# The longest neighbour lists of a graph kernel, laid out by rank, with a limit of places for each rank

## Chip, core and metric

The kernel runs on one core of one Trainium2 chip. The metric is the time of one execution on the device in microseconds (us), the median of several runs. Lower is better.

## What is computed

There are B = 16 graphs of N = 1024 nodes with C = 64 channels, a weighted adjacency `adj` (16, 1024, 1024) in float32 that is mostly zero, and a node mask (all ones). The reference, cut to what matters:

```python
# layer 0
h = relu(layernorm(x));  x = x + (adj @ h) / max(adj.sum(2), 1)
# layer 1
h = relu(layernorm(x))
nb = (adj > 0) without the diagonal;  m = nb.sum(-1)           # m: length of a node's list
skip = where(m > 10, (m + 1) // 2, 1)                          # every skip-th neighbour is removed
removed = nb & (skip > 1) & (rank_in_row % skip == 0)
valid = adj_with_self_loops without (removed or removed^T)
agg = sum of 1/4, 1/2, 1/4 times the quantiles .25, .5, .75 of h over the valid neighbours, by channel
x = x + relu((h + agg) @ W1 + b1) @ W2 + b2
```

The costly part is the quantile: for every node the feature rows of its neighbours (its list) have to be fetched and sorted in each of 64 channels. Lists are short on average and a few are long: the expected length of node i falls as 1 / sqrt(1 + i); the longest list of the inputs has 78 neighbours, and from the 512th of a graph on they have 3 or fewer.

## The kernel before, in words

**Two paths.** `list_path` does the whole work with lists. It also collects overflow flags (`ovf`): a list longer than the places set aside for it raises one. At the end the flags are reduced to `go`, and if it is set `dense_path` does everything again without lists. The trace shows `list_path` alone.

**Stages of `list_path`.** For each graph the rows of `adj` are loaded, layer 0 is computed (transposes and products on TensorE), and the neighbours are listed: `listing` finds the 8 largest keys in each of 4 segments of a row. `endings` (L737) then sorts the nodes of a graph by the length of their lists, only roughly: up to 15 by the length itself, and above that by the classes of `STEPS` = (16, 20, 24, 32) (L30, L764: one VectorE instruction for each step and graph). Inside a class the nodes keep their order. From the class counts each node gets a place `pos`, and a GpSimd indirect DMA (`scatter`) writes its record of 164 floats to the sorted table `srt` of its group of four graphs: 8 scatters for each graph, 128 in all. The four graphs are mixed in runs of eight ranks: eight ranks of the first graph, then eight of the second, and so on.

**Short jobs.** `group` (L1102) takes 32 tiles of 128 sorted nodes of four graphs. Tiles of the same limit form a `Job` (L831). A job fetches, for each tile t and each place k, one neighbour's row (66 floats) for each of the 128 nodes with one indirect DMA: `gather(A[:, k + 1, t, :], table, idx[:, t, k:k+1])`; `A` is named `places`. Then VectorE sorts the places with a min/max network, ScalarE and VectorE weight them, TensorE adds them up and runs the two matrix products, and one scatter for each tile writes `out`. The last group runs in the long stage (names with `last_`).

**Long lists.** The 32 longest lists of each graph (the first tile of each group) do not fit the record of 32 keys. `long_lists` (L1239) takes them again as four tiles l = 0 to 3 of 128 lists: 8 ranks of each of the 16 graphs, ranks 0 to 7 in l = 0. `LONG` (L40) = (88, 31, 24, 20) is the number of places of each tile, the same for all its partitions. For a tile, in this order: the records are loaded into `lS` (four DMAs on SP, one for each group, 32 partitions each, L1251); `lnodes` is made from them on VectorE; the rows of `adj` are gathered (`lat`); VectorE lists and sorts the keys (`lfound`, `lkeys`), raises the flags, applies the skip rule (`dilation`) and writes the fetch indices `lidx`; a `Job` with one tile fetches the K places from `whole`, the table of all graphs. For l = 0 the job's tile is `lplaces0` [128, 89, 1, 66], with 88 fetches of 128 rows each. Partition p holds graph p >> 3, rank p & 7. A list shorter than 88 fetches a row of huge numbers for its empty places.

**What sets the order.** All instructions go through `Plan` (L234 to L333). Each stream of work (`endings`, `group`, `Job.run` and so on) is a generator that names the engine it wants next and the time from which it can go on; `Plan.run` always takes the stream that could start first by a clock of its own and by rank. The clock has costs by engine, written into `note` (L271): a gather or scatter counts 1.27, a VectorE memset 0.04, a DMA issue on SP 0.05, whatever their size. The order on each engine is thus fixed when the program is built, and an engine that waits holds up all that stands behind the waiting instruction in its queue. On GpSimd (POOL) and VectorE (DVE) this order is the program's order.

The trace puts nearly every instruction on line L228, the helper that records it; instructions are found by the names of their tiles.

Of the kernel before, what the change touches and what calls it, by code (L numbers as in the profile page):

```python
# [9 lines left out]
F32 = mybir.dt.float32  # L10
BF = mybir.dt.bfloat16
HF = mybir.dt.float16
I32 = mybir.dt.int32
U8 = mybir.dt.uint8
AF = mybir.ActivationFunctionType
OP = mybir.AluOpType
AX = mybir.AxisListType

P = 128
# [4 lines left out]
HUGE = 1.0e30  # L24
# [2 lines left out]

GROUPS = (4, 4, 4, 4)
NSEG = 4
STEPS = (16, 20, 24, 32)  # L30
CLS = 15 + len(STEPS) + 1


# [4 lines left out]
)  # L38
CAPS2 = [CAPS[1]] + CAPS[2::2]
LONG = (88, 31, 24, 20)  # L40
LSEG = 8
LCAPS = (24, 16, 16, 16)
LSUB = 8
# [190 lines left out]
class Plan:  # L234
# [25 lines left out]
    def room(self, name, bufs):  # L260

        tiles = self.slots.get(name, ())
        if len(tiles) < bufs:
            return 0.0
        old = tiles[-bufs]
        return INF if self.users[old] else max(self.used.get(old, 0.0), self.ready.get(old, 0.0))

    def at(self, *tiles):
        return max(self.ready.get(t.tensor.name, INF) for t in tiles)
# [104 lines left out]
def list_path(ctx, tc, x, adj, nodemask, w1, b1, w2, b2, out, go):  # L374
    nc = tc.nc
    B, N, C = x.shape
# [5 lines left out]
    NG = len(GROUPS)  # L382
    FIRST = [sum(GROUPS[:g]) for g in range(NG)]
    TS = N + 1
# [59 lines left out]
    nc.vector.tensor_scalar(toff, which, float(TS), None, op0=OP.mult)  # L444
    noff = consts.tile([P, 3], F32, name="noff")
    nc.vector.tensor_scalar(noff, which, float(N), None, op0=OP.mult)
    caps4 = consts.tile([P, NTAU], F32, name="caps4")
    for t, cap in enumerate(CAPS):
        nc.vector.memset(caps4[:, t:t + 1], float(cap if t else N))
# [362 lines left out]
    def gather(dst, src, idx):  # L812
        nc.gpsimd.indirect_dma_start(
            out=dst, out_offset=None, in_=src,
            in_offset=bass.IndirectOffsetOnAxis(ap=idx, axis=0),
        )
# [14 lines left out]
    class Job:  # L831
# [1 line left out]


        def __init__(self, pool, n, T, keys, idx, node, mask, nodes_i, table, S, g, name="places",
                     bufs=4, rank=0, half=False, begin=0.0):
            self.__dict__.update(locals())
            self.short = pool is gat

        def run(self):  # L840
            n, T, pool, short = self.n, self.T, self.pool, self.short

            since = []
            own = () if short else (lambda rank: self.rank,)
            pace = lambda: since[0] + 1.3 * len(since) if not short else 0.0
            yield "POOL", lambda: max(
                self.begin, at(self.idx), room(self.name, self.bufs), room("S", 4) if short else 0.0
            ), *own
            A = self.A = new(pool, [P, n, T, W], F32, self.name, self.bufs, users=1)
            progress["ahead"] += T * (n - 1)  # L850
            if short:
                mine = self.S
                self.S = new(pool, [P, T, C], F32, "S", 4, users=1)
                nc.sync.dma_start(self.S, mine[:, :, :C])
                self.residual = mine[:, :, X1:R0]
            for t in range(T):
                for k in range(n - 1):
                    if t or k:
                        yield "POOL", pace, *own
                    since.append(since[0] if since else plan.clock["POOL"])  # L860
                    plan.own = plan.clock["POOL"]
                    gather(A[:, k + 1, t, :], self.table, self.idx[:, t, k:k + 1])
                    plan.own = None
                    progress["ahead"] -= 1
            yield "DVE", lambda: max(
                at(A, self.S) + SLACK,
                *(room(("" if short else "l") + name, 2 if short else 1) for name in ("gone", "wu")),
            ), self.soon
            yield from self.sort()
# [369 lines left out]
    def long_lists(pool):  # L1239

        yield "DVE", always
        rev = new(pool, [P, N], HF, "rev", 1)
        nc.vector.tensor_scalar(rev, col_f, -1.0, float(N), op0=OP.mult, op1=OP.add)
        for l, K in enumerate(LONG):
            n = K + 1
            yield "SP", always
            S = new(pool, [P, 1, RW], F32, "lS", 4)
            for g in range(NG):
                lo, num = FIRST[g] * LSUB, GROUPS[g] * LSUB
                at0 = l * num + (0 if GROUPS[g] == 4 else HP)  # L1250
                nc.sync.dma_start(  # L1251
                    S[lo:lo + num, 0, :], srt[g][at0:at0 + num, :]
                )
            node = S[:, 0, RW - 2:RW - 1]
            mask = S[:, 0, RW - 1:RW]
            yield "DVE", lambda: at(S) + SLACK if progress["begun"] == NG else INF
            nodes = tiny.tile([P, 1], F32, name="lnodes")
            nc.vector.tensor_tensor(nodes, node, noff[:, 1:2], OP.add)
            nodes_i = new(pool, [P, 1], I32, "lnodes_i", 4)
            nc.vector.tensor_copy(nodes_i, nodes)  # L1260
            yield "POOL", lambda: max(at(nodes_i), room("lat", 1))
            full = new(pool, [P, N], F32, "lat", 1)
            gather(full, adj_rows, nodes_i)
            yield "DVE", lambda: at(full)
            nc.vector.scalar_tensor_tensor(
                full, col_f, node, full, op0=OP.not_equal, op1=OP.mult
            )
            key = new(pool, [P, N], HF, "lkey", 1)
            nc.vector.scalar_tensor_tensor(key, full, 0.0, rev, op0=OP.is_gt, op1=OP.mult)

            found = new(pool, [P, LSEG, max(LCAPS)], HF, "lfound", 1)
            found = found[:, :, :LCAPS[l]]
            last = [None] * LSEG
            for r in range(LCAPS[l] // 8):
                for s in range(LSEG):
                    if s % 4 == 0:
                        yield "DVE", always
                    top = found[:, s, 8 * r:8 * r + 8]
                    seg = key.rearrange("p (q s) -> p s q", s=LSEG)[:, s, :]
                    if r:  # L1280
                        nc.vector.match_replace(
                            out=seg, in_to_replace=last[s], in_values=seg, imm_value=0.0
                        )
                    nc.vector.max(out=top, in_=seg)
                    last[s] = top
            rounds = -(-K // 8)
            keys = new(pool, [P, 1, rounds * 8 + 8], F32, "lkeys", 4)
            over = new(pool, [P, 2], F32, "lover", 1)
            nc.vector.tensor_reduce(over[:, 0:1], found[:, :, LCAPS[l] - 1], AX.X, OP.max)
            for r in range(rounds + 1):  # L1290
                if r % 4 == 0:
                    yield "DVE", always
                top = keys[:, 0, 8 * r:8 * r + 8]
                nc.vector.max(out=top, in_=found)
                if r < rounds:
                    nc.vector.match_replace(
                        out=found, in_to_replace=top, in_values=found, imm_value=0.0
                    )
            nc.vector.tensor_tensor(over[:, 1:2], over[:, 0:1], keys[:, 0, K:K + 1], OP.max)
            nc.vector.tensor_scalar(  # L1300
                ovf[:, NG + l:NG + l + 1], over[:, 1:2], 0.0, None, op0=OP.is_gt
            )
            keys = keys[:, :, :K]
            pos = new(pool, [P, K], F32, "lpos", 4)
            m = tiny.tile([P, 1], F32, name="lm")
            nc.vector.tensor_scalar(
                pos, keys[:, 0, :], 0.0, None, op0=OP.is_gt, op1=OP.add, accum_out=m
            )
            skip = dilation(m, mask, 1)
            for e in range(2):  # L1310
                nc.vector.tensor_scalar(pos, place1[:, :K], skip[:, e, :], None, op0=OP.not_equal)
                nc.vector.tensor_tensor(keys[:, 0, :], keys[:, 0, :], pos, OP.mult)
            based = tiny.tile([P, 1], F32, name="lbased")
            nc.vector.tensor_scalar(based, toff[:, 1:2], float(N), None, op0=OP.add)
            idx = new(pool, [P, K], I32, "lidx", 4)
            index_of(idx, keys[:, 0, :], -1.0, based)

            yield "DVE", lambda: 0.0 if progress["groups"] == NG else INF
            job = Job(
                pool, n, 1, keys, idx.unsqueeze(1), node, mask, nodes_i, whole, S, NG,  # L1320
                *(("lplaces", 2) if l else ("lplaces0", 1)), -600 + l, begin=at(whole),
            )
            plan.add(job.run(), 100 * NG + l)

# [309 lines left out]
```

## Time and profile before

| | |
|---|---|
| time, median of 3 runs | 1953.29 us (1948.59 to 1955.87) |
| profiled execution: span from the first to the last instruction | 1511.0 us |
| median less span: what lies around the span | 442.3 us |
| busy in the span: PE, DVE, ACT, POOL | 49%, 79%, 54%, 63% |
| indirect DMAs on POOL | 931 |
| of them: `lplaces`, all four long tiles | 163, first at 953.8 us |
| first step of the long sort (`lrem` of l = 0) | 1096.5 us |
| mean granted TensorE clock | 0.699 |

The page has busy time by engine, and busy tenths in 40 slices of 37.8 us each. "Busy" for an indirect DMA on POOL is the time in which POOL makes the transfer; the data land later. In a row of the timeline the columns are start, duration, engine, line, operation, output<-input, and in brackets the idle time of the engine just before, with what ended it. "issue" there means that the engine waited for nothing that the profile shows. In a row of the waits the columns are the total, the number of times, and the longest. In a row of the windows each engine has its busy us and, in brackets, its instructions.

### The profile page before, as it was taken

Reading aid. Unit: us, or ns where it says so; the run is one execution under the profiler, and the core shown is the slowest. Engines: PE = TensorE matmul, PEld = TensorE weight load, DVE = VectorE, ACT = ScalarE, POOL = GpSimd, SP = SyncE. Lnnn points to the kernel's source line nnn. Section 1 sums busy time; section 2 is a strip of 40 time slices with the busy share of each in tenths; the row PEclk is TensorE's granted clock in tenths of the full one; section 3 lists DMA queues with packets and bytes.
Section 4 is the critical chain, followed back from the end, with each engine's and each line's share of the span. In section 5 each row is a group of like instructions: output and inputs, shape, how many; then the busy total and the mean of one; then the engine's idle time right before and its main releaser. Section 6 shows DMA issues by size and latency. Waiting matters only on the chain. (4 is left out here: it accounts for less than half of the span.)

```text
span 1511.0 us, 15983 instructions
## 1 busy us (share of the span) xinstructions
PE 738.8 (49%) x3192; PEld 464.7 (31%) x3192; DVE 1191.3 (79%) x4104; ACT 816.4 (54%) x2789; POOL 957.2 (63%) x1154
## 2 busy tenths in 40 slices
PE   4778777327877556567667620024000123228542
PEld 2434334214544233343444320012000122216432
DVE  6777798997899779859869869893059999986875
ACT  7989878557879457757975520201050223148341
POOL 0122227777678757757777787667777777765083
PEclk8889888658888777869688755555555565558765
DMA  5445665424355253355341242111111111211010
GB/s 177 150 142 168 163 210 160 123 73 114 101 162 152 59 174 94 99 126 161 94 140 31 60 101 68 50 37 28 30 26 23 28 28 40 44 33 22 2 25 13
DMA packets 135718, 133.36 MB, mean 88 GB/s; under 512 B 100756, under 2 KB 103444, under 8 KB 135492
## 3 DMA queue, kind: packets, MB, share of 16 engines
q1 hardware_dynamic: 102876, 90.79, 20.8%
q0 software_dynamic: 32736, 41.47, 11.2%
q14 instruction: 78, 0.64, 0.1%
q8 instruction: 28, 0.46, 0.1%
HBM read 112.90 MB, written 23.61 MB: 90 GB/s over the span
## 5 line engine op out<-in xcount | busy, mean ns | idle before, releaser
L228 POOL DMA_INDIRECT places<-tab,idx x372 | 370.2, 995 | 131.7 <-issue 101.8
L228 PE MATMUL pt<-ident,prod 128*128 128x128 f32 (+1 forms) x736 | 160.2, 377 | 517.8 <-DVE prod L228 241.2
L228 PEld LDWEIGHTS pt<-ident,prod 128*128 128x128 f32 (+1 forms) x736 | 129.3, 256 | 550.4 <-ACT prod L228 412.4
L228 PE MATMUL ps_small<-att,h 128*65 128x512 f32 x512 | 254.7, 644 | 27.3 <-ACT h L228 10.5
L228 POOL DMA_INDIRECT srt<-row,to x128 | 125.9, 984 | 165.8 <-ACT row L228 144.0
L228 PE MATMUL pt<-ident,at 128*128 128x128 f32 x1024 | 176.7, 320 | 96.0 <-ACT att L228 71.1
L228 POOL DMA_INDIRECT lplaces<-whole,lidx x163 | 167.2, 1026 | 55.6 <-issue 48.5
L228 DVE MAX8 rec<-sg 128x8 f16<-128x256 f16 x512 | 180.1, 414 | 4.4
L228 PEld LDWEIGHTS pt<-ident,at 128*128 128x128 f32 x1024 | 136.9, 164 | 143.5 <-ACT att L228 93.8
L228 ACT ACTIVATE sg<-at 128x1024 f16<-128x1024 f32 x128 | 134.8, 1054 | 75.0 <-DMA at<-in_adj_dram 65.7
L228 ACT COPY att<-pt 128x512 f32<-128x512 f32 x256 | 141.9, 582 | 20.7 <-PE pt L228 18.8
L228 POOL DMA_INDIRECT places<-tab,last_idx x124 | 123.8, 998 | 41.3 <-issue 35.0
L228 PEld LDWEIGHTS ps_small<-att,h 128*65 128x65 f32 x512 | 74.7, 151 | 161.9 <-issue 123.2
L228 ACT ACTIVATE places<-places,gone 128x64 f32<-128x64 f32 x496 | 123.5, 335 | 0.5
L228 ACT ACTIVATE prod<-places,w 128x64 f32<-128x64 f32 x213 | 54.1, 336 | 120.5 <-DVE w L228 120.5
L228 POOL DMA_INDIRECT out_dram<-y,nodes_i x93 | 91.8, 987 | 22.6 <-issue 15.1
L228 DVE TENSOR_TENSOR sg<-sg,keyed 128x1024 f16<-128x1024 f16 x128 | 87.2, 681 | 23.7 <-ACT sg L228 23.7
L228 ACT ACTIVATE gone<-gone 128x15 f32<-128x15 f32 (+9 forms) x40 | 8.2, 206 | 169.2 <-DVE ok L228 169.0
L228 DVE TENSOR_TENSOR long_other<-lplaces 128x512 f32<-128x512 f32 (+5 forms) x124 | 64.1, 555 | 29.1 <-ACT lplaces L228 28.9
L228 DVE TENSOR_TENSOR other<-places,other 128x64 f32<-128x64 f32 (+6 forms) x204 | 69.6, 341 | 5.9
L228 PE MATMUL ps_small<-ot,w_sb 128*128 128x128 f32 (+3 forms) x112 | 47.6, 513 | 44.2 <-DVE y L228 31.2
L228 DVE TENSOR_TENSOR places<-places,other 128x64 f32<-128x64 f32 (+2 forms) x208 | 62.3, 309 | 4.9
(231 smaller groups left out, 1670.8 us busy)
## 6 DMA issues: line engine op xcount, KB each, us to landing
at<-in_adj_dram SPq DMA_DIRECT2D x128, 512.0 KB
places<-tab,idx POOLq DMA_INDIRECT x372, 2.5
whole<-tab SPq DMA_DIRECT2D x4, 1057.0 KB
tab<-row SPq DMA_DIRECT2D x16, 264.0 KB
xt<-in_x_dram SPq DMA_DIRECT2D x16, 256.0 KB
lplaces<-whole,lidx POOLq DMA_INDIRECT x163, 2.4
srt<-row,to POOLq DMA_INDIRECT x128, 2.7
places<-tab,last_idx POOLq DMA_INDIRECT x124, 2.4
```

The costliest lines, as they stand in the source:

```text
L228: ins = getattr(self._engine, op)(*args, **kwargs)
```

## The change

1. `STEPS` gets two more classes, 40 and 52, so that the longest lists of a graph stand nearer to their order of length. `CLS` follows (20 to 22).
2. The tile of l = 0 is laid out by rank: partition p now holds graph p & 15, rank p >> 4. Its records are loaded with 32 DMAs of 4 partitions (one for each group and rank) in place of 4 DMAs of 32. New constants (`toff0`, `noff0`, `rcaps`) follow this layout.
3. `RCAPS` = (88, 82, 80, 54, 46, 44, 37, 35) is the limit of places of each rank. A list over the limit of its rank raises the flag.
4. The fetch of place k takes only the partitions of the ranks whose limit is over k: 128 for the first 35 places, 16 for the last six.
5. What is not fetched is filled by one memset of `lplaces0` from place 36 on (53 places of 66 floats for each partition). For this the tile is allocated in `long_lists` and handed to the job.

```diff
-STEPS = (16, 20, 24, 32)
+STEPS = (16, 20, 24, 32, 40, 52)
+RCAPS = (88, 82, 80, 54, 46, 44, 37, 35)
...
+    ranked = consts.tile([P, 2], I32, name="ranked")
+    nc.vector.tensor_scalar(ranked[:, 0:1], part, B - 1, None, op0=OP.bitwise_and)
+    nc.vector.tensor_scalar(ranked[:, 1:2], part, B.bit_length() - 1, None, op0=OP.logical_shift_right)
...
+    for r in range(1, LSUB):
+        nc.vector.tensor_scalar(
+            rstep, ranked[:, 1:2], float(r), float(RCAPS[r - 1] - RCAPS[r]), op0=OP.is_lt, op1=OP.mult
+        )
+        nc.vector.tensor_tensor(rcaps, rcaps, rstep, OP.add)
...
+            longest = self.name == "lplaces0"
...
-                    gather(A[:, k + 1, t, :], self.table, self.idx[:, t, k:k + 1])
+                    top = B * sum(cap > k for cap in RCAPS) if longest else P
+                    gather(A[:top, k + 1, t, :], self.table, self.idx[:top, t, k:k + 1])
...
-                nc.sync.dma_start(
-                    S[lo:lo + num, 0, :], srt[g][at0:at0 + num, :]
-                )
+                if l:
+                    nc.sync.dma_start(S[lo:lo + num, 0, :], srt[g][at0:at0 + num, :])
+                    continue
+                ranks = srt[g][at0:at0 + num, :].rearrange("(b r) w -> r b w", r=LSUB)
+                for r in range(LSUB):
+                    lo = r * B + FIRST[g]
+                    nc.sync.dma_start(S[lo:lo + GROUPS[g], 0, :], ranks[r])
...
+            A = None
+            if not l:
+                nc.vector.tensor_tensor(over[:, 0:1], m, rcaps, OP.is_gt)
+                nc.vector.tensor_tensor(
+                    ovf[:, NG:NG + 1], ovf[:, NG:NG + 1], over[:, 0:1], OP.max
+                )
+                A = new(pool, [P, n, 1, W], F32, "lplaces0", 1, users=1)
+                nc.vector.memset(A[:, min(RCAPS) + 1:, :, :], HUGE)
```

More of the change, by code (lines that the diff above doesn't have):

```diff
@@ L446, in list_path @@
     nc.vector.tensor_scalar(noff, which, float(N), None, op0=OP.mult)
+    ranked = consts.tile([P, 2], I32, name="ranked")
+    nc.vector.tensor_scalar(ranked[:, 0:1], part, B - 1, None, op0=OP.bitwise_and)
+    nc.vector.tensor_scalar(ranked[:, 1:2], part, B.bit_length() - 1, None, op0=OP.logical_shift_right)
+    toff0 = consts.tile([P, 1], F32, name="toff0")
+    nc.vector.tensor_scalar(toff0, ranked[:, 0:1], float(TS), None, op0=OP.mult)
+    noff0 = consts.tile([P, 1], F32, name="noff0")
+    nc.vector.tensor_scalar(noff0, ranked[:, 0:1], float(N), None, op0=OP.mult)
+    rcaps = consts.tile([P, 1], F32, name="rcaps")
+    nc.vector.memset(rcaps, float(RCAPS[-1]))
+    rstep = consts.tile([P, 1], F32, name="rstep")
+    for r in range(1, LSUB):
[3 more added lines that the diff above has]
+        nc.vector.tensor_tensor(rcaps, rcaps, rstep, OP.add)
     caps4 = consts.tile([P, NTAU], F32, name="caps4")
@@ L835, in __init__ @@
         def __init__(self, pool, n, T, keys, idx, node, mask, nodes_i, table, S, g, name="places",
-                     bufs=4, rank=0, half=False, begin=0.0):
+                     bufs=4, rank=0, half=False, begin=0.0, A=None):
             self.__dict__.update(locals())
@@ L846, in run @@
             yield "POOL", lambda: max(
-                self.begin, at(self.idx), room(self.name, self.bufs), room("S", 4) if short else 0.0
+                self.begin, at(self.idx), room("S", 4) if short else 0.0,
+                at(self.A) if self.A is not None else room(self.name, self.bufs),
             ), *own
-            A = self.A = new(pool, [P, n, T, W], F32, self.name, self.bufs, users=1)
+            A = self.A = (
+                new(pool, [P, n, T, W], F32, self.name, self.bufs, users=1)
+                if self.A is None else self.A
+            )
             progress["ahead"] += T * (n - 1)
@@ L1250, in long_lists @@
                 at0 = l * num + (0 if GROUPS[g] == 4 else HP)
-                nc.sync.dma_start(
-                    S[lo:lo + num, 0, :], srt[g][at0:at0 + num, :]
-                )
+                if l:
[5 more added lines that the diff above has]
+                    nc.sync.dma_start(S[lo:lo + GROUPS[g], 0, :], ranks[r])
+            toffs, noffs = (toff[:, 1:2], noff[:, 1:2]) if l else (toff0, noff0)
             node = S[:, 0, RW - 2:RW - 1]
@@ L1257, in long_lists @@
             nodes = tiny.tile([P, 1], F32, name="lnodes")
-            nc.vector.tensor_tensor(nodes, node, noff[:, 1:2], OP.add)
+            nc.vector.tensor_tensor(nodes, node, noffs, OP.add)
             nodes_i = new(pool, [P, 1], I32, "lnodes_i", 4)
@@ L1308, in long_lists @@
             )
+            A = None
[3 more added lines that the diff above has]
+                    ovf[:, NG:NG + 1], ovf[:, NG:NG + 1], over[:, 0:1], OP.max
+                )
+                A = new(pool, [P, n, 1, W], F32, "lplaces0", 1, users=1)
+                nc.vector.memset(A[:, min(RCAPS) + 1:, :, :], HUGE)
             skip = dilation(m, mask, 1)
@@ L1313, in long_lists @@
             based = tiny.tile([P, 1], F32, name="lbased")
-            nc.vector.tensor_scalar(based, toff[:, 1:2], float(N), None, op0=OP.add)
+            nc.vector.tensor_scalar(based, toffs, float(N), None, op0=OP.add)
             idx = new(pool, [P, K], I32, "lidx", 4)
@@ L1320, in long_lists @@
                 pool, n, 1, keys, idx.unsqueeze(1), node, mask, nodes_i, whole, S, NG,
-                *(("lplaces", 2) if l else ("lplaces0", 1)), -600 + l, begin=at(whole),
+                *(("lplaces", 2) if l else ("lplaces0", 1)), -600 + l, begin=at(whole), A=A,
             )
```

## The prediction

> **What bounds the kernel now.** I read the page's busy tenths first, to see where which engine is full, then busy time by windows around the long lists, then the waits of that window, then the timeline around the start of the long stage. On the page (40 slices of 37.8 us):
>
> ```profile
> DVE  6777798997899779859869869893059999986875
> POOL 0122227777678757757777787667777777765083
> ```
>
> Counted from 0, POOL stands at about 7 from slice 6 to 34. That is full: an indirect DMA is busy for 0.944 us and begins 1.25 us after the one before, the rest being 0.30 us of "issue" each time. So POOL sets the pace until the long stage. VectorE has one hole, in slices 27 to 29 (digits 3, 0, 5). The windows show it, and what comes behind it:
>
> ```profile
> 243.00:890.00 647.00, 404.47 (x1688) 249.33 (x1687) 536.00 (x1880) 440.59 (x1498) 477.21 (x591) 0.75 0.40 110
> 954.00:1096.50 142.50, 24.88 (x92) 16.07 (x92) 72.32 (x240) 19.66 (x73) 103.81 (x120) 0.54 0.15 37
> 1096.50:1511.00 414.50, 125.20 (x668) 100.75 (x668) 336.65 (x1107) 145.44 (x579) 265.87 (x291) 0.60 0.12 26
> ```
>
> The columns are PE, PEld, DVE, ACT, POOL. In the second row VectorE is busy for 72 of 142 us, in the third for 337 of 414. The wait that ends the hole, and what VectorE waits for after it (waits of VectorE from 1096 us on):
>
> ```profile
> DVE lrem L228 <- DMA lplaces<-whole,lidx: 50.1, 2, 48.9
> DVE long_other L228 <- ACT lplaces L228: 28.9, 9, 5.7
> DVE y L228 <- PE ps_small L228: 14.0, 3, 5.7
> DVE other L228 <- ACT places L228: 13.6, 3, 11.2
> ```
>
> Of the 50.1 us, 48.9 are one wait: the sort of l = 0 starts at 1096.5 us, when the last of its 88 fetches has landed. After that VectorE waits for ScalarE and TensorE and only 1.2 us for a fetch. So **the end is the arrival of l = 0 plus some 414.5 us of VectorE's queue**, and the change is worth what it does to that arrival, less VectorE work that it takes out of the 414.5. What fixes the arrival is the chain at the start of the stage (timeline, SP, DVE and POOL):
>
> ```profile
> 890.78 0.36 SPq L228 DMA_DIRECT2D last_recs<-srt  x1
> 891.19 9.82 SPq L228 DMA_DIRECT2D lS<-srt  x16
> 896.48 0.26 DVE L228 CAST last_nodes_i<-nodes 128x32 int32<-128x32 f32 x1
> 897.44 0.16 DVE L228 TENSOR_TENSOR lnodes<-lS,noff 128x1 f32<-128x1 f32 x1 [0.71 <-DMA lS<-srt]
> 952.51 0.94 POOL L228 DMA_INDIRECT lat<-in_adj_dram,lnodes_i  x1 [1.47 <-DVE lnodes_i L228]
> ```
>
> The records are loaded as soon as the last scatter to `srt` (ends 889.2) has landed; `lnodes` of l = 0 waits for its four loads (0.71 us more than for `last_recs`). From there VectorE runs without a gap (54.5 us) to the `lnodes_i` of l = 1 behind the indices of l = 0, and POOL waits for it (1.47 us) before the first fetch at 953.8.
>
> **Part by part.** All against the profiled execution, span 1511.0 us. The median of the runs is 1953.3, so 442.3 us lie around the span; I leave them as they are and add the change of the span to the median.
>
> *Order, +10.* The plan is built anew. By the order of instructions, 531 indirect DMAs stand on POOL up to the last `srt` scatter, against 523 before: eight more at 1.25 us. POOL's queue is the pace there. Cover would be POOL's named waits from 270 us to that scatter, 40 us (12.3 for y, 9.3 for `row`, 9.2 and 7.1 for ScalarE, 2.2): if the eight fall into them the term is 0, and these waits can come out 10 us longer or shorter in a new order.
>
> *Loads, +11.* 32 loads stand where 4 stood, and `lnodes` in the new order waits for all of them. The price of one issue on SP: (9.82 - 2.85) / 15 = 0.465 us in the `lS` row (its first takes 2.85), at the other end the short loads
>
> ```profile
> 3.12 1.20 SPq L464 DMA_DIRECT2D b_sb<-in_L_gnn_b_dram  x4
> ```
>
> at 0.30. At 0.40: 31 x 0.40 - 3 x 0.465 = 11.0 (bounds 7.9 and 13.0). Behind the waiting `lnodes` in VectorE's queue stand the listing of the last group, whose `drop` lets `whole` be written, and the whole listing of l = 0; POOL's `lat` waits for `lnodes_i` with 36 DMAs behind it. Those 36 take 45 us, VectorE's chain 54.5, so POOL catches up and the chain stays what sets the start.
>
> *Memset and flag, +3.4.* They stand in that same chain, ahead of the indices. Two tiny instructions at 0.2, and a memset of 53 x 66 = 3498 elements. Rows:
>
> ```profile
> L228 DVE MEMSET keys<- 128x512 f32 x3 | 1.5, 485 | 0.2
> L228 DVE MEMSET prod<- 128x320 f32 x4 | 1.3, 325 | 7.3 <-PE pt L228 7.3
> ```
>
> (485 - 325) / 192 = 0.83 ns an element, so 0.485 + 2986 x 0.00083 = 2.97 us. The fetches behind it have no further wait.
>
> *More scatters inside the fetches, +7.6.* Between the first and the last fetch of the tile POOL now has 20 scatters to `out`, before 14: 6 x 1.27. (Nine more short fetches stand ahead of the first one; they are in POOL's slack against the chain.)
>
> *Fetches, -10.* There are still 88, so what counts is whether one with fewer rows is shorter. Sum over the limits: 16 x 466 = 7456 rows in place of 11264, 3808 fewer, in 53 of the 88. No row of the trace has an indirect DMA of fewer than 128 rows. The nearest:
>
> ```profile
> L228 POOL DMA_INDIRECT lplaces<-whole,lidx x163: 940/944/1782, 953.8 to 1459.9; - x163
> L228 POOL DMA_INDIRECT lat<-in_adj_dram,lnodes_i x4: 942/942/960, 902.2 to 1001.6; - x4
> ```
>
> 264 bytes a row and 4096 bytes a row take the same 0.94, so bytes are not what it pays for; rows or a fixed part are. Below: nothing saved, 0. Above: all of the 0.944 by rows, 7.4 ns x 3808 = 28.1, and with the 0.30 of issue too, 37.1. I take 10, a third of 28: the rows nearest to it say only that the time does not move with the size. The Trainium skill speaks against the change here: "DMA: Bandwidth & Descriptors", section "Anatomy of one DMA — SWDGE (gpsimd) path", calls the descriptor generation small and says that many descriptors can be emitted before their cost shows. By it this term would be 0 and the sum 10 us higher; the trace, with one row count alone, can neither confirm nor deny it.
>
> *Work moved ahead of the arrival, -7.2.* In the new order one more short job (6 tiles of 2 places) and six `y` stand on VectorE before the sort of l = 0: 6 small instructions at 0.2, some 7 at 0.55, a 0.4, two at 0.18 and 6 `y` at 0.21, 7.2 us. They fill part of the 48.9 us hole.
>
> *Nothing.* 32 more step instructions (0.167 each, 5.3 us) and a tenth more elements in the class sums (about 1.3): hidden by POOL's pace; uncovered, 6.6. Nineteen small constants (3.6 us) at the start: mostly in VectorE's wait of 2.5 us for the first `adj`. The listing, sort and layers of l = 0 keep their shapes.
>
> Sum: 10 + 11 + 3.4 + 7.6 - 10 = +22 for the arrival, less 7.2 behind it: **+15, span 1526, time 1968 us**, 0.8% slower. The tail after the arrival has its own order (VectorE waits some 56 us there for ScalarE and TensorE); I give it 8 us either way.
>
> **Rivals.**
>
> *A fetch costs the same whatever its rows.* For it: bytes do not move it. Then the term of 10 is 0: +25, 1978.
>
> *A fetch is busy by its rows.* For it: 0.94 us is long beside POOL's bare instructions (0.12 for a one-element memset). Then -28 in place of -10: -3, 1950, no difference that a measurement of this kernel tells (its runs spread over 7 us; 0.5%, 10 us, is my bound).
>
> *The loads are hidden.* If `last_recs` or the engine's own queue is late by as much, `lnodes` loses nothing: +4, 1957, the same. Against it: `last_recs` came 1.2 us before `lnodes` could go, and nothing else stood between.
>
> *Faster.* One mechanism: the whole pitch of a fetch, issue included, goes by its rows. Place: the 53 shortened fetches; price 9.7 ns a row, 37 us; -12, 1941. It decides from a saving of 25 + 10 = 35 us on, 9.2 ns a row. Against it: the 0.30 of issue is the same ahead of every kind of indirect DMA.
>
> *The change does not hold on these inputs.* A list over its limit would run `dense_path`, with 16 x 64 x 8 x 18 matmuls; at the 0.32 us of the cheapest group of the page that is over 47 ms. From the reference's inputs the longest lists by rank in the new order are 78, 58, 51, 38, 38, 31, 31, 27, all under `RCAPS`.
>
> **How the numbers follow.** Forecast (saving 5 to 20) 0.45, of which 0.35 lies over +0.5%; fixed cost 0.22; by rows 0.12; hidden loads 0.08; faster 0.12; dense 0.01. So slower 0.35 + 0.22 + 0.01 = 0.58, same 0.10 + 0.12 + 0.08 = 0.30, faster 0.12. The range takes in a saving of 37 (1941) and of 0 with the order 10 us worse (1988): 1940 to 1990.
>
> **What would show it.** `lnodes` waits 10 to 13 us on the DMAs of `lS`; the last `srt` scatter ends near 899; the memset of `lplaces0` takes about 3 us; the busy time of the fetches of 48 and 16 rows against 0.944 decides among the rivals; `lrem` of l = 0 starts near 1118 and the span ends some 407 us later. The forecast is wrong if the last `srt` scatter comes early, if short fetches take under 0.6 us, or if the tail after `lrem` changes by over 10 us.

## The result, and the profile after

The kernel after takes 1964.2 us (median of 6 runs, 1959.7 to 1973.4) against 1953.2 us before (1948.6 to 1956.3): **ratio 1.006, 95% interval 1.0036 to 1.0085**, 11 us slower. The forecast was 15 us slower.

The size came out by chance, as the next lines show. Span and busy tenths of VectorE and POOL, from the page of the kernel after (a slice is now 49 us):

```profile
span 1959.0 us, 16074 instructions
...
DVE  7875945776653872756357736793100699885674
...
POOL 0122365454556546437453566467677114563152
```

This execution's time was 1960.8, so only 1.8 us lie around its span. The 442 us that the prediction "left around the span" are not there; POOL is not full from slice 6 to 34, and VectorE's hole is one weakness among many.

The experiments ran in three sets, each on one chip with the kernel before beside it, and the kernel before takes 1952.6 us on the first, 1985.0 on the second and 1517.2 on the third; so only ratios and stages within one set are compared. By their times, and by nothing else, the profile of before that the prediction read (span 1511) is counted with the third set, and the median that it was added to, with the runs of the kernel after above, with the first.

### The profile page after: what moved, and what is told of

It reads as the page before. It is cut to its first block, busy times and chain, and to the rows that moved or that the text cites. A ratio compares the mean times of both kernels' runs of the same rounds, so it can differ in the third digit from the quotient of the medians.

```text
span 1959.0 us, 16074 instructions
## 1 busy us (share of the span) xinstructions
PE 804.9 (41%) x3192; PEld 506.1 (26%) x3192; DVE 1204.9 (62%) x4158; ACT 832.6 (42%) x2791; POOL 939.6 (48%) x1158
## 4 chain that ended last, share of the span: by engine, by line
DVE 30%; ACT 18%; issue 16%; another core or an unknown queue 13%; PE 12%; POOL 6%; DMA 2%; SPq 1%; DVEq 0%; POOLq 0%; ACTq 0%
PE pt L229 6%; PE ps_small L229 6%; DVE other L229 5%; DVE places L229 5%; DVE long_other L229 4%; DVE lplaces L229 3%; ACT sg L229 3%; POOL lplaces L229 3%; ACT att L229 2%; ACT places L229 2%; ACT ln_sq L229 2%; DVE rec L229 2%; ACT lplaces L229 2%; POOL places L229 2%
## 5 line engine op out<-in xcount | busy, mean ns | idle before, releaser
L229 POOL DMA_INDIRECT places<-tab,idx x372 | 364.4, 980 | 242.9 <-issue 108.4
L229 PE MATMUL pt<-ident,prod 128*128 128x128 f32 (+1 forms) x736 | 172.8, 398 | 598.6 <-DVE prod L229 313.0
L229 PE MATMUL pt<-ident,at 128*128 128x128 f32 x1024 | 201.7, 350 | 267.2 <-ACT att L229 108.6
L229 PEld LDWEIGHTS pt<-ident,prod 128*128 128x128 f32 (+1 forms) x736 | 139.0, 274 | 633.8 <-ACT prod L229 408.7
L229 POOL DMA_INDIRECT srt<-row,to x128 | 126.1, 985 | 244.6 <-ACT row L229 208.7
L229 PEld LDWEIGHTS pt<-ident,at 128*128 128x128 f32 x1024 | 152.4, 180 | 317.3 <-ACT att L229 130.7
L229 POOL DMA_INDIRECT lplaces<-whole,lidx x163 | 155.9, 956 | 56.6 <-issue 48.4
L229 ACT COPY ot<-pt 128x128 f32<-128x128 f32 (+3 forms) x56 | 22.2, 397 | 200.6 <-remote 132.7
L229 DVE TENSOR_TENSOR sg<-sg,keyed 128x1024 f16<-128x1024 f16 x128 | 87.3, 682 | 12.5 <-ACT sg L229 9.3
L229 PE MATMUL ps_small<-ot,w_sb 128*128 128x128 f32 (+3 forms) x112 | 52.9, 564 | 76.9 <-ACT ot L229 41.3
```

Of the source, the lines that this page charges most:

```text
L229: ins = getattr(self._engine, op)(*args, **kwargs)
```

## Experiments

### e0: the kernel before, profiled again (first set)

No edit.

> The kernel before, unchanged, profiled again. The profile that the prediction read had a span of 1511 us, and the prediction left 442 us around it. If they do lie around the span, this profile again has a span near 1511, with lrem of l = 0 near 1096. The rival: that execution was one in which the waits that fill the timed runs did not occur; then the span here is within a few us of the time, about 1951, as in the profile of the kernel after (span 1959.0 in a run of 1960.8), lrem of l = 0 starts near 1400, and the chain holds 'issue' and 'remote' shares of over 10%.

Measured: 1947.6 us, span 1945.7. From its page:

```profile
span 1945.7 us, 15983 instructions
...
PE 798.3 (41%) x3192; PEld 503.5 (26%) x3192; DVE 1194.1 (61%) x4104; ACT 832.2 (43%) x2789; POOL 941.8 (48%) x1154
```

VectorE is busy for 1194 us here and for 79% of 1511, 1191 us, in the first profile: VectorE's work is the same, and the 435 us are idle time. (TensorE is busy 60 us longer, 798.3 against 738.8, at a mean granted clock of 0.641 against 0.699.) Part of the idle time stands ahead of instructions that wait for nothing on this core: "issue", or "remote", a release that the profile cannot name. Summed over the waits of the whole span, these two come to 482 us on ScalarE and 180 on VectorE in e0, and to none and 3 us in the first profile. The rest of VectorE's added idle time is longer waits for ScalarE and TensorE. The gaps show best in the 88 ScalarE activations that begin the sort of l = 0 (timelines of ScalarE; first the profile with a span of 1511, then e0):

```profile
1097.78 21.10 ACT L228 ACTIVATE lplaces<-lplaces,lgone 128x64 f32<-128x64 f32 x88
```

```profile
1389.73 5.59 ACT L228 ACTIVATE lplaces<-lplaces,lgone 128x64 f32<-128x64 f32 x23
...
1470.56 0.35 ACT L228 ACTIVATE lplaces<-lplaces,lgone 128x64 f32<-128x64 f32 x1 [1.05 <-issue]
1471.96 0.35 ACT L228 ACTIVATE lplaces<-lplaces,lgone 128x64 f32<-128x64 f32 x1 [1.05 <-issue]
```

The same instructions begin every 0.24 us in the one, and after the first 23 mostly every 1.40 us in the other, with nothing that they wait for ("issue"). The rival holds; lrem starts at 1388.5, as it expected, but the large "issue" and "remote" shares in the chain did not appear (1% each: the chain that the page gives is short). So the prediction's profile was a sound picture of the kernel, but under conditions that its timed runs did not have.

### e1: all rows fetched (first set)

```diff
-                    top = B * sum(cap > k for cap in RCAPS) if longest else P
+                    top = P
```

> The kernel after, but every fetch of the longest list takes all 128 rows again. In the profile of the kernel after a fetch of 128 rows is busy for 0.944 us and one of 16 rows for about 0.85, 0.8 ns a row. By the rival of the prediction in which a fetch costs nearly the same whatever its rows, this kernel is 3 us slower than the one after (1967). By the forecast (saving of 10) 1974; with the fetches paid by rows (saving of 28) 1992.

Measured: 1970.0 us, 1.0064 of before (1.0038 to 1.0091). Against the 1.006 of the kernel after, the intervals overlap almost wholly: a saving of 28 us is excluded, one of 3 cannot be resolved by the time. The durations can (timeline of POOL in the kernel after; the fetches of 128, 48 and 16 rows):

```profile
1258.28 0.94 POOL L229 DMA_INDIRECT lplaces<-whole,lidx  x1 [0.30 <-issue]
...
1340.87 0.88 POOL L229 DMA_INDIRECT lplaces<-whole,lidx  x1 [0.30 <-issue]
...
1417.04 0.85 POOL L229 DMA_INDIRECT lplaces<-whole,lidx  x1 [0.30 <-issue]
```

An eighth of the rows still takes 90% of the time. In the two profiles the stretch from the first fetch to `lrem` is 171.9 us in e1 and 161.1 in the kernel after, but POOL is busy for only 2.2 us less there; 8.4 of the 10.8 us are a scatter's wait for `y` of VectorE (22.0 and 13.6 us in total). So that difference is not the price of the rows.

### e2 and e3: the two halves of the change (first set)

e2 is the kernel before with the new classes alone, e3 the kernel after with the old ones:

```diff
-STEPS = (16, 20, 24, 32)
+STEPS = (16, 20, 24, 32, 40, 52)
```

> The kernel before with the six STEPS of the kernel after and nothing else. The prediction's order term says +10 (1963): the new plan puts eight more indirect DMAs ahead of the last srt scatter. Rival: POOL is not what paces that stage in the timed executions (48% busy there), so the order term is within 5 us of 0 (1948 to 1958).

> The kernel after with the four STEPS of the kernel before: the layout by rank, its 32 loads, the memset and the shortened fetches remain. The prediction's terms without order: loads +11, memset +3.4, fetches -10, so about +5 (1958). Rival from the profile of the kernel after (lnodes waits 14.6 us for the loads, fetches save 3): +14 and +3 less 3, so 1967, if the start of the long stage sets the end; if it does not, 1953.

Measured: **e2 1973.5 us, 1.0101 (1.0073 to 1.0129); e3 1945.3 us, 0.997 (0.9945 to 0.9994).** The whole loss sits in the two classes, by twice the order term; layout, 32 loads, memset and short fetches together are not a loss of 5 or 14 us but a small gain, against both theories. Two things limit what e3 says. From the last scatter to `lrem` it takes as long as e0 (244.9 and 244.6 us); what it gains is behind `lrem` (548.9 against 557.2). And its new plan also moves work: a job marks the empty places of a tile on ScalarE, or, when the plan's clock says that ScalarE is late, in one instruction on VectorE. In e3 the last long tile goes the second way: 20 ScalarE activations are replaced by one VectorE instruction of 1.5 us. That tile takes 44.3 us from its `lrem` to the end of the span, 61.1 in e0 and 52.5 to 53.5 in the kernel after, e1 and e2. So the gain is not shown to be the layout's.

### e4: 32 loads alone (second set)

```diff
-                nc.sync.dma_start(
-                    S[lo:lo + num, 0, :], srt[g][at0:at0 + num, :]
-                )
+                step = num if l else GROUPS[g]
+                for k in range(0, num, step):
+                    nc.sync.dma_start(
+                        S[lo + k:lo + k + step, 0, :], srt[g][at0 + k:at0 + k + step, :]
+                    )
```

> The kernel before with the records of l = 0 loaded in 32 pieces of 4 rows instead of 4 of 32; the order on VectorE, ACT, PE and POOL is the same to the instruction. The prediction's loads term says +11 (1964). The rival, from the profiles of e0 and e3: behind lnodes VectorE had some 20 us of 'issue' gaps in the kernel before (39.7 us from lnodes to the first operation on lat) and none behind the longer wait (19.9 us), so the wait for 32 loads fills idle time that is there anyway: 0 to +3 (1953 to 1956), lnodes again waits about 14 us and lat follows it by 20.

Measured: 1977.1 us, **0.9962 of before (0.9939 to 0.9985)**: the added wait does not cost 11 us, the kernel is 7 faster. Waits of VectorE from lnodes to the first operation on lat, in e6 below (order of before, four loads, same set) and in e4:

```profile
DVE last_keys L229 <- issue: 17.0, 16, 1.9
DVE left L229 <- remote: 2.5, 1, 2.5
DVE lnodes L229 <- DMA lS<-srt: 0.9, 1, 0.9
```

```profile
DVE lnodes L228 <- DMA lS<-srt: 15.3, 1, 15.3
DVE half L228 <- DVE half L228: 1.3, 1, 1.3
```

With four loads VectorE goes on after 0.9 us and then loses 19.5 in gaps of about 1 us inside the listing of the last group. With 32 it waits 15.3 us and then runs that listing without them. From the last scatter to the first fetch the two take nearly the same, 87.9 us in e4 and 86.9 in e6. The wait stands in the place of gaps that were there anyway. That explains 0; why the gaps close behind a wait, and why the time comes to less than 0, is not shown.

### e5 and e6: order and work of the classes apart (second set)

In e5 the plan is told of two more steps and the larger sums, so that VectorE and POOL stand in the order of e2, but they do the work of four steps; in e6 the reverse. Only these two engines follow the plan's order. On ScalarE and TensorE some 30 and 14 instructions of e5 stand elsewhere than in e2, and some 55 and 67 of e6 elsewhere than in before. The core of the edits:

```diff
             for s in STEPS[1:]:
                 nc.vector.scalar_tensor_tensor(d, total, float(s), d, op0=OP.is_gt, op1=OP.add)
+            for _ in range(2):                                  # e5
+                plan.note("DVE", "scalar_tensor_tensor", (d, total, 0.0, d), {})
```

```diff
-                nc.vector.scalar_tensor_tensor(d, total, float(s), d, op0=OP.is_gt, op1=OP.add)
+                step = (tc.nc if s > 32 else nc).vector.scalar_tensor_tensor   # e6
+                step(d, total, float(s), d, op0=OP.is_gt, op1=OP.add)
```

> The kernel before (four STEPS), with its plan told that there are six: VectorE and POOL carry their instructions in the order of the kernel with six STEPS (e2), and do the work of four. If the new order is the cost of STEPS, about 1973 as e2, with the last srt scatter at 1167 to 1175 as in e2 and after. If the added instructions are the cost, 1953 with the last scatter near 1145. The prediction's term had both in one, +10.

> The other half: six STEPS (32 more small instructions on VectorE, a tenth more elements in the class sums) in the order of the kernel before with four. If the order is the cost: 1953, at most 1960 (6.6 us of uncovered work by the prediction). If the added instructions are the cost: about 1973.

Measured: e5 1987.3 us, 1.0008 (0.9977 to 1.004); e6 1983.3 us, 0.9995 (0.9969 to 1.0021). Neither half costs what e2 cost in the first set. By e6 the added instructions alone cost at most 0.2% on this chip, in an order of ScalarE and TensorE that is not quite that of before; for the order alone the runs leave at most 0.4%. The stages of e5 do carry the mark of the order: first fetch to `lrem` is 171.1 us, as in e2 (170.8), against 158.8 in e6 and e4, and the last `srt` scatter ends at 1189, against 1170 in e6 and 1181 in e4. But the profiled executions of e5 and e4 took 17 and 15 us more than their medians, so the latter does not decide.

### e7: single costs (second set)

```python
def acts():
    for k in range(K):                      # K = 120
        nc.scalar.activation(a[:, k, :], a[:, k, :], AF.Identity, bias=zero)
for top in (128, 112, 96, 80, 64, 48, 32, 16):
    g = fetches(f"rows{top}", top, 10)      # ten indirect DMAs of top rows
    step(g)                                 # the next stage waits for all of them
```

> Not the reference's computation: the output is x itself; only single costs are measured. 120 ScalarE activations of 128x64 first alone, then while POOL issues 120 fetches of 128 rows, then while it issues 120 of 16 rows; then ten fetches each of 128, 112, 96, 80, 64, 48, 32 and 16 rows. By the profile of the kernel after, a fetch takes 0.94 us at 128 rows and 0.85 at 16, so 0.8 ns a row over 0.84 fixed; by the forecast's term it would fall to 0.79 at 16 rows or less. If the gaps of 1.05 us between ScalarE's instructions in the long stage come from the fetches that POOL issues beside them, an activation begins every 0.24 us alone and every 0.7 or 1.4 us beside the 128-row fetches; if they come from something else, every 0.24 in all three.

Measured, median busy time of ten fetches by rows (the pitch is 0.30 more):

| rows | 128 | 112 | 96 | 80 | 64 | 48 | 32 | 16 |
|---|---|---|---|---|---|---|---|---|
| us | 0.94 | 0.93 | 0.91 | 0.90 | 0.90 | 0.87 | 0.86 | 0.84 |

(0.94 - 0.84) / 112 = 0.9 ns a row over 0.83 fixed. The 3808 rows that the change leaves out are worth 3.4 us. ScalarE ran at 0.24 us an activation alone and beside the 128-row fetches; beside the 16-row ones (timeline of ScalarE):

```profile
412.84 4.88 ACT L47 ACTIVATE acts<-acts,zero 128x64 f32<-128x64 f32 x20 [303.17 <-DVE zero L70]
420.10 0.35 ACT L47 ACTIVATE acts<-acts,zero 128x64 f32<-128x64 f32 x1 [2.38 <-issue]
...
427.83 0.35 ACT L47 ACTIVATE acts<-acts,zero 128x64 f32<-128x64 f32 x1 [1.04 <-ACT acts L47]
429.23 0.35 ACT L47 ACTIVATE acts<-acts,zero 128x64 f32<-128x64 f32 x1 [1.05 <-ACT acts L47]
```

Twenty go fast; after a few uneven steps the rest begin every 1.40 us, as in e0. It is the third run of 120, so this is about 260 activations into ScalarE's program. Larger fetches are not the reason, since the 128-row ones beside the second run did no harm; whether it is the small ones or the place in the program, this run cannot tell, because the two came together.

### e8 to e10: the same question on the third chip

e8 is e2 again, e9 the kernel after unchanged. e10 is e3 with the memset moved ahead:

```diff
+            A = None
+            if not l:
+                yield "DVE", always
+                A = new(pool, [P, n, 1, W], F32, "lplaces0", 1, users=1)
+                nc.vector.memset(A[:, min(RCAPS) + 1:, :, :], HUGE)
             yield "DVE", lambda: at(S) + SLACK if progress["begun"] == NG else INF
```

> The kernel of e2 once more (the kernel before with six STEPS), because e2 said +1.0% of before while its two halves (e5: order, e6: work) each said 0.0% in another set of runs. If the two together cost what neither does alone, about 1.010 again. If +1% belonged to that set of runs, within 0.4% of before here.

> The kernel after, unchanged, beside e8 on the same chip. With the first result 1.006 again, and below e8 by what the layout gives (e3: -0.4%; loads alone in e4: -0.4%; shortened fetches in e1: -0.3%): so about 0.5% below e8. If e8 is within 0.4% of before, this one is at or below before.

> The version that the runs point to: layout by rank and shortened fetches with the four STEPS of before (e3), and the memset of lplaces0 moved to where VectorE waits for the loads of l = 0 anyway. The memset took 2.97 us ahead of the indices in the profiles of after and of e3. Relative to e3 (0.997 of before): 3 us less, so 0.995, if the chain of VectorE still sets the first fetch; 0.997 if the gaps in VectorE's instructions take the 3 us back.

Measured, before 1517.2: **e8 1540.9 us, 1.0142 (1.0119 to 1.0164); e9 1546.4 us, 1.0191 (1.0174 to 1.0208); e10 1515.6 us, 0.9984 (0.9967 to 1.0).** On this chip the change costs 29 us. Its classes again carry most of it (24), but here the layout adds 5 where in the first set it took 9 away. e10 is level with before; e3 did not run in this set, so the times do not tell what the early memset gives. The stages do: in e10 it ends inside the wait for the loads, which is no longer for it (10.38 us against 10.40 in e9), and `lnodes` to the first fetch is 55.3 us in place of 60.2 (56.8 in e8, which has no memset). The version that beat both kernels is e3, on the first chip. e10 has the same 20 activations replaced as e3: it reaches `lrem` 7.9 us later after the last scatter than before does (215.2 against 207.3), and its tail is 8.3 us shorter (406.2 against 414.5), with no wait for ScalarE in the last long tile where before has 5.7.

Here the executions look like the profile that the prediction read. Windows of the profile of before, last scatter to `srt` to `lnodes`, then to the first fetch of l = 0 (columns PE, PEld, DVE, ACT, POOL busy, in brackets the instructions; then granted clock, DMA share, GB/s):

```profile
889.00:897.40 8.40, 7.31 (x33) 5.71 (x32) 1.44 (x4) 1.27 (x2) 6.38 (x9) 0.70 0.69 111
897.40:953.80 56.40, 0.00 (x0) 0.00 (x0) 53.29 (x201) 0.22 (x1) 42.97 (x46) 0.50 0.29 78
```

and of e9, the same two, then first fetch to `lrem`, then `lrem` to the end:

```profile
908.00:925.70 17.70, 7.28 (x32) 5.69 (x31) 1.24 (x3) 1.27 (x2) 10.32 (x11) 0.60 0.54 101
925.70:985.90 60.20, 0.00 (x0) 0.00 (x0) 56.41 (x203) 0.16 (x1) 38.16 (x39) 0.50 0.21 50
985.90:1133.40 147.50, 34.76 (x136) 23.85 (x136) 79.22 (x263) 28.61 (x106) 107.69 (x131) 0.55 0.15 31
1133.40:1548.90 415.50, 132.56 (x624) 105.72 (x624) 329.56 (x1085) 139.10 (x555) 249.16 (x270) 0.57 0.13 24
```

### e11: are the gaps the program's? (third set)

```python
for beside in (None, P, None, P, None, 16, None, 0, None):   # 0: plain loads
    if beside == 0: slabs()
    elif beside: fetches(beside)
    acts()                                                   # 100 activations
    step()
```

> Not the reference's computation: the output is x itself; nine stages of 100 ScalarE activations of 128x64, each begun when the stage before has ended: alone, beside 128-row fetches of POOL, alone, beside 128-row fetches, alone, beside 16-row fetches, alone, beside plain loads of 512 KB on SP, alone; then three stages of 100 VectorE operations: alone, beside fetches, alone. In e7 activations began every 0.24 us alone and beside 128-row fetches, and every 1.40 beside 16-row fetches from their 21st on, some 260 instructions into ScalarE's program. If POOL's fetches slow the others' instructions once a first store of instructions is used up: 0.24 in all stages alone, 1.4 in the stages beside fetches of either size from the third on, 0.24 beside plain loads. If it is the length of the program alone: 1.4 in every stage from the third on.

Measured: 0.24 us an activation in all nine stages, beside fetches or not (the first 38 of the 100 of the sixth stage, beside 16-row fetches):

```profile
456.12 9.17 ACT L51 ACTIVATE acts<-acts,zero 128x64 f32<-128x64 f32 x38 [30.32 <-DVE zero L75]
```

Neither theory holds on this chip: no stage is slow. It is the chip whose kernel before takes 1517 us. e7's own program was not run here, but the kernel before was, and it has the gaps on two chips and not on this one. So they are not a property of an instruction stream alone; they come with the set of runs.

## Why the prediction was right, and where it was not

Stages in us from the start of the span, from the timelines (one execution each):

| kernel, set | last `srt` scatter | `lnodes` | first op on `lat` | first fetch, l = 0 | `lrem` | span |
|---|---|---|---|---|---|---|
| before, the profile read | 889 | 897.4 | 916.3 | 953.8 | 1096.5 | 1511.0 |
| e10, third | 896 | 913.9 | 933.1 | 969.2 | 1111.1 | 1517.3 |
| e8, third | 907 | 916.5 | 935.8 | 973.3 | 1123.7 | 1540.4 |
| e9 (after), third | 908 | 925.7 | 944.7 | 985.9 | 1133.4 | 1548.9 |
| e0 (before), first | 1144 | 1152.6 | 1192.3 | 1230.2 | 1388.5 | 1945.7 |
| e2, first | 1175 | 1183.5 | 1222.6 | 1261.4 | 1432.2 | 1970.5 |
| e3, first | 1155 | 1177.7 | 1197.6 | 1243.3 | 1400.4 | 1949.3 |
| after, first | 1167 | 1189.7 | 1209.2 | 1258.3 | 1419.4 | 1959.0 |

On POOL, e10 and e3 have the order of before up to the last scatter and reach it 7 and 11 us later: a difference of 10 us between two profiles there is by itself no finding.

**Under the conditions that it assumed (e9, e8 against the profile read), by its own steps:**

- *Order, +10.* +19 (908 against 889), of which 10 are the term as it was forecast. The eight added DMAs all stand between the 120th and the last `srt` scatter: POOL makes 27 indirect DMAs there in e8 and e9, 19 in before and e10, and takes 34.4 us in e8 and e9, 24.2 and 24.3 in before and e10. The windows of this stretch, before and e9 (the last pair, x31 and x42, counts all of POOL's instructions, the small ones too):

```profile
864.00:889.20 25.20, 6.22 (x23) 4.84 (x23) 15.76 (x44) 11.64 (x50) 20.64 (x31) 0.50 0.24 61
872.20:907.60 35.40, 9.23 (x37) 4.75 (x36) 17.10 (x46) 12.70 (x52) 28.73 (x42) 0.63 0.30 67
```

  The other 8 us are there at the 120th scatter already (872 against 864), where e10, with POOL's order of before, is as late (871); they are not shown to be the order's.
- *Loads, +11.* 17.7 against 8.4 us from the last scatter to `lnodes`: +9.3, and the wait at `lnodes` is 10.4 where before had 0.7. SP issues the 32 loads in 13.6 us, 0.42 each. Right. (The row names the load that SP issued next; in e10 the same wait is named `lS<-srt`.)

```profile
925.74 0.16 DVE L229 TENSOR_TENSOR lnodes<-lS,noff 128x1 f32<-128x1 f32 x1 [10.40 <-DMA S<-srt]
978.76 2.97 DVE L229 MEMSET lplaces<- 128x3498 f32 x1 [0.68 <-issue]
```

- *Memset and flag, +3.4.* 60.2 against 56.4: +3.8. The memset took 2.97 (the second row above), as worked out from the two other memsets. Right.
- *Six scatters, +7.6.* e8, with full fetches, has 150.4 from first fetch to `lrem` against 142.7: +7.7. Right.
- *Fetches, -10.* 147.5 (e9) against 150.4 (e8): -2.9. **This step failed**: a third of the time by rows was taken, and it is about an eighth (0.9 of 7.4 ns). The rival of a fixed cost was nearly true.
- *Moved work, -7.2.* **This step failed in its result.** VectorE's busy time behind `lrem` did fall from 336.65 to 329.56 us, by 7.1, but the stretch did not get shorter (415.5 against 414.5). The waits of VectorE in this stretch in e9 name what came late next; the first line stood at 28.9 in before:

```profile
DVE long_other L229 <- ACT lplaces L229: 40.0, 11, 8.4
DVE y L229 <- PE ps_small L229: 12.5, 2, 7.3
```

  The 11.1 us that were added are mostly waits of the tiles l = 1 and 2 for ScalarE (two of 4.9 and 2.7 us, and one of 8.4 where before had 5.6). e8, the classes alone, has the same 40.0 us, so they come with the order of the classes. The prediction gave the tail 8 us either way; this took all of them.

The sum there is +38 between the two spans and +29 between the medians of the third set, not +15. The 9 us between these two fit the spread of executions: e9's profiled one took 4 us more than its median, and a span of 1511 is 4 us short of what the median of before leaves.

On the fetch, the Trainium skill ("DMA: Bandwidth & Descriptors", section "Anatomy of one DMA — SWDGE (gpsimd) path") calls descriptor generation small within the fixed cost of a DMA. The measured 0.9 ns a row, 0.1 us of POOL's 0.94 for all 128, agrees with that; the prediction weighed it and took the larger value all the same.

**In the timed runs (after against e0)** the same terms come out otherwise:

- *Order:* +23 at the last scatter in this pair, +31 in e2. Here POOL is busy for 48% and does not pace: from the 120th to the last scatter the eight added DMAs cost 3 us (45.1 against 41.8), because waits for VectorE and ScalarE of 18 us become 12. The larger part arises between the 40th and the 120th scatter (868.0 us, 872.4 in e2, against 851.0). What it is there is not shown; e3, without the classes, is 8 us longer there too.
- *Loads:* the wait at `lnodes` is 14.6 us, more than forecast, but `lnodes` to the first operation on `lat` falls from 39.7 to 19.5. From the last scatter to the first fetch it is +5 with the memset included. **The term of +11 failed**, because the chain "without a gap (54.5 us)" has gaps of some 20 us in these runs which the wait replaces. e4 shows it alone. The rival of hidden loads had the price nearly right and the mechanism wrong: `lnodes` does wait, and it is the gaps behind it that go.
- *Fetches and scatters:* first fetch to `lrem` 161.1 against 158.3: +2.8, near 7.6 - 3.4, but by chance: with full fetches e2 and e1 have +12.5 and +13.6, and 7 to 8 us of what lies between is a shorter wait for `y`, not the rows.
- *Tail:* 539.6 against 557.2, -17.6, where -7.2 were expected. 7.3 of it is VectorE work (windows of the two profiles: 337.5 and 330.2); the other 10 is idle time, whose part in the gaps is not taken apart. e2 has -18.9 without the layout, so the classes brought it.

Sum +13 in the profiles, +11 in the medians. The forecast of +15 was met because its errors cancel: the order was 13 too small and the saving of the fetches 5 too large, loads and memset were 9 too dear, and the tail gave back 10 more than it was given. What decided were the two classes: without them the kernel is no slower than before on two chips (e3 0.997, e10 0.998), helped in both by the 20 activations that the plan moved to VectorE, and in e10 by the early memset.

**What stays open.** By e2 and e8 the classes cost 1.0 and 1.4%. On the third chip the parts of this are seen: 10 us for the eight DMAs and 7.7 for the six scatters. On the first it is not known why they cost 21 us. e5 and e6, the two halves, showed no cost on the second chip, where the whole was not run. What opens the gaps of 1.05 us on two chips and not on the third is not known either.

## What to carry to other kernels

Compare span and time first: if hundreds of microseconds lie between them (442 here, 1.8 in the kernel after), the profile may be of an execution unlike those that were timed, and a second profile is worth more than any sum. A wait added ahead of a chain cost next to nothing where the chain behind it had gaps that closed in its place (e4); the tight chain paid nearly all of it (e9). Work moved out of the last stretch need not shorten it: in e9 it waited for the engine that hands over there, ScalarE. A change of a plan that orders everything also moves work that it does not name, as the 20 activations of e3 and e10; count the instructions by tile on each side before a time is put down to the edit.

## What had not been expected of the hardware

- The same program, with the same busy time (VectorE 1191 and 1194 us), took 1517 us on one chip and 1953 and 1985 on two others. The difference on VectorE is idle time, in gaps ahead of instructions that wait for nothing that the profile shows, and in the waits for other engines that have such gaps.
- The gaps keep to a grid: ScalarE's activations of 0.35 us begin 0.70, 1.40 or 2.10 us apart (in e0, 42 of the 63 slow steps of the 88 are at 1.40, 13 at 0.70 and 5 at 2.10). They start after 20 to 23 fast activations.
- The Trainium skill ("Runtime: NRT & Kernel Launch", section "Instruction fetch mechanics") says that an engine's instructions come in blocks of 256 and that the cost of going from one to the next is mostly hidden. In e7 the gaps began about 260 activations into the program and then met every instruction; in e11, with 900, there were none. That the gaps are instruction supply is argued, not shown.
- An indirect DMA of 16 rows is busy for 0.84 us, one of 128 for 0.94: with 0.30 of issue, leaving out seven eighths of the rows saves 8% of the time from one fetch to the next.
